# Graph attention on one core: a quarter of the weighting of gathered rows on ScalarE, with the weights in SBUF

## The chip, the core and the metric

The kernel runs on one core of one Trainium2 chip. A core has five engines with instruction queues of their own, each worked off in order: PE (TensorE: matrix products, with PEld for its weight loads), DVE (VectorE), ACT (ScalarE), POOL (GpSimd, which here issues the gathers by index) and SP (which here issues plain transfers). They wait for each other through semaphores. The metric is the device time of one execution in microseconds.

## The reference

One layer over 6250 nodes of 256 features, in three parts. The change lies in the first, a graph attention over 200 000 edges that are sorted by destination:

```python
z = jnp.einsum('ni,hid->nhd', h, W)              # 4 heads of 64
es = jnp.einsum('nhd,hd->nh', z, a_src)
ed = jnp.einsum('nhd,hd->nh', z, a_dst)
e = es[src] + ed[dst]
e = jnp.where(e >= 0, e, SLOPE * e)
ex = jnp.exp(e - m[dst])                         # m: maximum over a node's edges
alpha = ex / denom[dst]                          # denom: sum of ex over a node's edges
out = jax.ops.segment_sum(alpha[:, :, None] * z[src], dst, num_segments=N)
```

Added to it are the node itself and a linear attention of 8 heads over all nodes (the mixer). A second part follows: a second, narrow graph attention over 131 072 other edges gives scores, which choose two of four experts for each node.

## The kernel before

**Tiles.** Nodes lie in 49 tiles of 128. Edges lie in chunks of 128, one edge a partition, at fixed places: 33 chunks for each tile but the last, which has 28. That makes 1612 chunks, worked off in 202 groups of `G1 = 8`. The table `ztab` in HBM holds for each node its `z` with a 1 behind every head (4 x 65 columns, `ZW`) and four source terms.

**First edge stage.** The class `FirstEdges` holds the steps of one group. `gather` (L784) issues on POOL one indirect transfer for each chunk: by the row numbers in `src_c` (SBUF) it brings 128 rows of `ztab` into the tile `gt`, which takes `GH = 4` chunks; there are seven such tiles. `load` (L807) brings the destination numbers from SP's queue. `one_hot` (L813) and `one_hot_t` (L822) build, on DVE, the 0/1 matrices between edges and nodes. `terms` (L828) fetches the destination terms by PE; `terms_sum` (L836), `sources` (L798, then two exponentials on ACT, L213 and L214) and `weights` (L840, L842) make of them four weights for each edge, `wp`. This array lies in PSUM, in the tile `dv`, whose first 128 columns hold the numbers 0 to 127. `weigh` (L848) multiplies half a group's gathered rows, 4 chunks x 4 heads x 65 columns, by the weights on DVE, in place, and `add` (L857) sums the rows by destination on PE, into the PSUM tile `ag` of the node tile.

**Order.** The loop over the groups writes out the order of every engine's queue. For group g: gathers of g+2, `load` of g+3, `weights`, `weigh` of chunks 0 to 3, `terms` of g+1, `add` of chunks 0 to 3, `weigh` of chunks 4 to 7, `one_hot` of g+1, `add` of chunks 4 to 7, `one_hot_t` of g+2, `terms_sum` and `sources` of g+1. In six places between these, `mix_hops` puts in steps of the mixer and of the second layer norm, which use PE, DVE, ACT and SP. At the end of a group come steps of the sorting of the second part's edges (L381, L383, L413, L415 on DVE).

**Second stage.** The same pattern for the second attention (`SecondEdges`, gathers at L1321), between the experts' matrix products (L1427, L1447). It is not touched. Neither is the other use of `FirstEdges`, a branch for inputs whose tiles hold more edges than the fixed places; the inputs here don't take it.

Of the kernel before, what the change touches and what calls it, by code (L numbers as in the profile page):

```python
# [9 lines left out]
F32 = mybir.dt.float32  # L10
# [3 lines left out]
AF = mybir.ActivationFunctionType  # L14
# [6 lines left out]
P = 128  # L21
# [6 lines left out]
G1 = 8  # L28
GH = 4
K1, K1L = 33, 28  # L30

ZW = 4 * 65
# [32 lines left out]
def gps_layer(ctx: ExitStack, tc: tile.TileContext, a: dict, out: bass.AP):  # L65
    nc = tc.nc
    V, S, G, T, SP = nc.vector, nc.scalar, nc.gpsimd, nc.tensor, nc.sync
# [431 lines left out]
    with tc.tile_pool(name="a_x", bufs=1) as ax, tc.tile_pool(name="a_w", bufs=3) as aw, tc.tile_pool(  # L499
        name="a_p", bufs=2, space=PSUM  # L500
# [269 lines left out]
    class FirstEdges:  # L770
# [67 lines left out]
        def weights(self):  # L838
            n, pw = self.n, self.pw
            V.tensor_mul(pw[:, :n], pw[:, :n], self.sf[:, :n])  # L840
            self.wp = self.dv[:, P : P + 4 * G1].rearrange("p (c h) -> p c h", h=4)
            V.tensor_max(self.wp[:, :n], pw[:, :n, 0:4], pw[:, :n, 4:8])  # L842

        def weigh(self, c0, c1):
            if c0 < self.n:
                c1 = min(c1, self.n)
                gz = self.gt[c0 // GH][:, : c1 - c0, 0:ZW].rearrange("p c (h d) -> p c h d", h=4)
                V.tensor_mul(gz, gz, self.wp[:, c0:c1].unsqueeze(3).to_broadcast([P, c1 - c0, 4, 65]))  # L848

        def add(self, sums, s0, c0, c1):  # L850

# [184 lines left out]
    with tc.tile_pool(name="g1_w", bufs=2) as w, tc.tile_pool(name="g1_g", bufs=7) as gp, tc.tile_pool(  # L1036
        name="m_w", bufs=2
# [78 lines left out]
    with tc.If(many != 0):  # L1116
# [7 lines left out]
        with tc.tile_pool(name="sl_k", bufs=1) as k, tc.tile_pool(name="sl_w", bufs=1) as w, tc.tile_pool(  # L1124
            name="sl_p", bufs=1, space=PSUM
# [41 lines left out]
            with tc.For_i(0, NI, 1) as i:  # L1167
                c = nc.values_load(
                    l_c[0:1, ds(i, 1)], engines=(ENG.SP,), min_val=0, max_val=B1 * P - 1,
                    skip_runtime_bounds_check_because="numbers of chunks",  # L1170
                )
# [66 lines left out]
    with tc.tile_pool(name="d_k", bufs=1) as dk:  # L1238
# [3 lines left out]
        with tc.tile_pool(name="d_o", bufs=1) as do:  # L1242
# [5 lines left out]
            with tc.tile_pool(name="s2_p", bufs=1, space=PSUM) as ps1:  # L1248
                room = acc2.rearrange("p t f -> p (t f)")
                source_max(do, ps1, most_2, h_all[:, :, HW:HF], "f2")  # L1250
                d = room[:, : NT * 4].rearrange("p (t h) -> p t h", h=4)
# [454 lines left out]
        with tc.tile_pool(name="g2_w", bufs=2) as w, tc.tile_pool(name="g2_g", bufs=6) as gp, tc.tile_pool(  # L1706
            name="g2_p", bufs=1, space=PSUM
# [88 lines left out]
        with tc.If(bad != 0):  # L1796

            own_edges()
            with tc.tile_pool(name="h2_k", bufs=1) as hk, tc.tile_pool(name="h2_w", bufs=1) as w, tc.tile_pool(
                name="h2_p", bufs=1, space=PSUM  # L1800
# [60 lines left out]
```

## Time and profile before

Three timed runs: 3212.33, 3219.29 and 3220.07 us; median 3219.29. The profiled execution took 4023.54 us, with a span of 4021.7 us from the first to the last instruction.

| | busy in the profile, us | share of the span | instructions |
|---|---|---|---|
| PE | 2498.4 | 62% | 10919 |
| DVE | 2464.6 | 61% | 6571 |
| POOL | 2328.2 | 58% | 2436 |
| ACT | 506.5 | 13% | 1319 |

| steps of the first edge stage | engine | count | mean ns |
|---|---|---|---|
| `weigh` L848 | DVE | 403 | 1224 |
| `one_hot` L813 | DVE | 202 | 1208 |
| `add` L857, two products a chunk | PE | 3224 | 474 |
| `weights` L842 | DVE | 202 | 190 |
| exponentials L213, L214 | ACT | 201 each | 321, 214 |

The first gather of the first edge stage starts at 138.1 us, its last at 2614.0; the second stage's gathers run from 2642.2 to 3957.9. In the rows of the profile, a group of instructions is named by line, engine, operation and tiles (out<-in), followed by shapes and count, then busy time and mean duration, then the idle time of the engine before them and what ended it. A row of the timeline has start and length in microseconds first. POOL's row for a gather is the time in which it issues one, not the transfer.

### The profile page before, as it was taken

The page shows a single profiled execution, that of the slowest core. Times are in us where ns is not written, and L with a number is a line of the kernel's source. Part 1 is how long each engine was busy: PE and PEld are TensorE (multiplying, and loading weights), DVE is VectorE, ACT ScalarE, POOL GpSimd, SP SyncE. Part 2 cuts the span into 40 slices and gives each one's busy share as a digit, 9 for nine tenths or more (in the row PEclk, how much of TensorE's full clock was granted, in tenths as well). Part 3 has the DMA queues.
Part 4 walks back from the last instruction along what each step waited for, and adds up shares of the span by engine and source line. Part 5 has one row for each costly group of instructions (what it writes and reads, how often), then busy time and mean ns, then how long its engine had stood idle before and what let it go on. Part 6 is the DMA issues. An engine that isn't in the chain of part 4 may idle for free. (4 is left out here: it accounts for less than half of the span.)

```text
span 4021.7 us, 36890 instructions
## 1 busy us (share of the span) xinstructions
PE 2498.4 (62%) x10919; PEld 1773.3 (44%) x10920; DVE 2464.6 (61%) x6571; ACT 506.5 (13%) x1319; POOL 2328.2 (58%) x2436
## 2 busy tenths in 40 slices
PE   5666677755564555546555555446666767677766
PEld 4444565544443444434444433324444444444444
DVE  5566666677774776766677566625555546565657
ACT  2200011111110110111111111121111011111112
POOL 2466666665665666656666566655556556555552
PEclk8778798877776777777777777767888788888878
DMA  5443344444443443444444444332222123222221
GB/s 166 131 114 109 108 116 110 119 119 116 122 130 97 116 123 108 120 112 115 133 116 127 113 125 109 104 81 51 45 60 50 42 49 81 53 61 57 59 56 32
DMA packets 248565, 388.33 MB, mean 97 GB/s; under 512 B 73447, under 2 KB 156279, under 8 KB 248090
## 3 DMA queue, kind: packets, MB, share of 16 engines
q0 software_dynamic: 103296, 230.96, 23.1%
q1 hardware_dynamic: 142893, 154.04, 12.6%
q8 instruction: 91, 1.49, 0.1%
q14 instruction: 129, 1.05, 0.1%
q10 hardware_dynamic: 2156, 0.80, 0.1%
HBM read 345.44 MB, written 40.15 MB: 96 GB/s over the span
## 5 line engine op out<-in xcount | busy, mean ns | idle before, releaser
L784 POOL DMA_INDIRECT gt<-ztab,src_c x1612 | 1551.5, 962 | 967.3 <-issue 406.3
L857 PE MATMUL ag<-gt,oh 128*128 128x260 f32 x3224 | 1017.2, 474 | 342.6 <-DVE gt L848 232.0
L1321 POOL DMA_INDIRECT gt<-htab,src x784 | 748.6, 955 | 595.3 <-DVE dv L1390 261.2
L857 PEld LDWEIGHTS ag<-gt,oh 128*128 128x128 f32 x3224 | 754.0, 241 | 527.2 <-DVE gt L848 255.0
L1427 PE MATMUL hp<-xy,w 128*128 128x512 f32 (+1 forms) x832 | 444.3, 657 | 187.2 <-ACT hT L1432 140.5
L1447 PE MATMUL yo<-w,hT 128*128 128x256 f32 x1568 | 446.4, 425 | 111.4 <-issue 63.8
L848 DVE TENSOR_TENSOR gt<-gt,dv 128x1040 f32<-128x1040 f32 x403 | 489.0, 1224 | 13.7 <-issue 12.6
L1447 PEld LDWEIGHTS yo<-w,hT 128*128 128x128 f32 x1568 | 316.5, 209 | 246.2 <-issue 137.2
L883 PE MATMUL m<-wqkv,xy 128*128 128x256 f32 (+1 forms) x784 | 254.6, 464 | 169.5 <-DVE kmax L894 85.3
L1427 PEld LDWEIGHTS hp<-xy,w 128*128 128x128 f32 x832 | 169.0, 216 | 328.5 <-issue 167.3
L883 PEld LDWEIGHTS m<-wqkv,xy 128*128 128x128 f32 (+1 forms) x784 | 171.8, 231 | 217.2 <-DVE kmax L894 91.3
L813 DVE TENSOR_TENSOR oh<-dv,dl_c 128x1024 f32<-128x1024 f32 x202 | 244.0, 1208 | 7.8 <-PE ag L857 5.2
L1432 ACT ACTIVATE hT<-hp,b 128x512 f32<-128x512 f32 (+1 forms) x208 | 133.5, 660 | 479.4 <-remote 172.9
L1371 DVE TENSOR_TENSOR e_sel<-ed,ohq 128x384 f32<-128x384 f32 x98 | 54.1, 552 | 182.4 <-remote 136.8
L213 ACT ACTIVATE src_f<-src_d,shift_c 128x32 f32<-128x32 f32 x202 | 64.9, 321 | 772.5 <-DVE src_d L798 441.4
L381 DVE MAX8 src<-dl 128x8 f32<-128x1024 f32 x128 | 155.5, 1215 | 0.0
L383 DVE MATCH_REPLACE8 dl<-src,dl 128x1024 f32<-128x1024 f32 x127 | 153.5, 1209 | 0.0
L976 PE MATMUL m<-m_sb,qT 128*128 128x256 f32 (+1 forms) x196 | 74.4, 516 | 125.4 <-ACT qT L973 86.8
L1412 DVE TENSOR_REDUCE ag<-ag 128x40 f32<-128x120 f32 x98 | 27.2, 277 | 193.5 <-remote 154.5
L828 PE MATMUL ed<-pw,ohT 128*128 128x24 bf16 x1612 | 71.8, 176 | 106.7 <-DVE ohT L822 46.3
L828 PEld LDWEIGHTS <-ohT 128*128 128x128 bf16 x1612 | 67.1, 100 | 141.6 <-DVE ohT L822 53.6
L836 DVE TENSOR_REDUCE pw<-ed 128x64 f32<-128x192 f32 x202 | 69.6, 344 | 94.9 <-remote 74.6
(374 smaller groups left out, 2745.7 us busy)
## 6 DMA issues: line engine op xcount, KB each, us to landing
br<-rows SPq DMA_DIRECT2D x299, 256.0 KB
gt<-ztab,src_c POOLq DMA_INDIRECT x1612
gt<-htab,src POOLq DMA_INDIRECT x784
early<-ys SPq DMA_DIRECT2D x24, 512.0 KB
ys<-early SPq DMA_DIRECT2D x24, 512.0 KB
ztab<-zt SPq DMA_DIRECT2D x48, 132.0 KB
row<-in_x_dram SPq DMA_DIRECT2D x48, 128.0 KB
out_dram<-ys SPq DMA_DIRECT2D x47, 128.0 KB
```

Of the source, the lines that this page charges most:

```text
L381: V.max(out=srtf[:, 8 * i : 8 * i + 8], in_=keyf)
L383: V.match_replace(out=keyf, in_to_replace=srtf[:, 8 * i : 8 * i + 8], in_values=keyf, imm_value=0.0)
L784: G.indirect_dma_start(out=self.gt[-1][:, c % GH, :], out_offset=None, in_=ztab[:, :], in_offset=bass.IndirectOffsetOnAxis(ap=self.idx[:, ...
L813: V.tensor_tensor(self.oh[:, :n], self.dv[:, None, :P].to_broadcast([P, n, P]), self.dl[:, :, None].to_broadcast([P, n, P]), op=OP.is_equal,)
L828: T.matmul(self.ed[:, c, :], self.ohT[:, c * P : (c + 1) * P], pw3[:, ds(self.tiles[c], 1), :].rearrange("p a b -> p (a b)"), start=True, ...
L848: V.tensor_mul(gz, gz, self.wp[:, c0:c1].unsqueeze(3).to_broadcast([P, c1 - c0, 4, 65]))
L857: T.matmul(sums[t], self.oh[:, c], self.gt[c // GH][:, c % GH, 0:ZW], start=(s0 + c == 0 or chunk_tile[s0 + c - 1] != t), stop=last,)
L883: T.matmul(out_, xy[:, t, j, :n], wqkv[:, j, c0 : c0 + D], start=(j == 0), stop=(j == 1))
L1321: G.indirect_dma_start(out=self.gt[:, c, : tab.shape[1]], out_offset=None, in_=tab[:, :], in_offset=bass.IndirectOffsetOnAxis(ap=self.idx[ ...
L1427: T.matmul(hp[:, :m], wts[e][0][:, c, j * P : (j + 1) * P], xy[:, t0 : t0 + nt, c] if m == nt * P else xy[:, t0, c, :m], start=(c == 0), s ...
L1432: S.activation(h[:, :m], hp[:, :m], AF.Gelu, bias=b1[:, e, j : j + 1])
L1447: T.matmul(yo[:n], hT[j][:, o : o + n], wts[e][1][:, j, :], start=(j == 0 and e < EARLY), stop=(j == 3))
```

## The change

Two edits in `FirstEdges`. The weights `wp` move from PSUM into an SBUF tile of their own, a single buffer. And `weigh` leaves the last chunk of every full half to ACT: DVE multiplies three chunks in one instruction (780 columns), ACT the fourth in four instructions, one for each head (65 columns, with the weight of the head as the scale of a `Copy` activation). All 403 halves are full, so ACT gets 1612 instructions.

```diff
         def weights(self):
             n, pw = self.n, self.pw
             V.tensor_mul(pw[:, :n], pw[:, :n], self.sf[:, :n])
-            self.wp = self.dv[:, P : P + 4 * G1].rearrange("p (c h) -> p c h", h=4)
+            self.wp = self.w.tile([P, G1, 4], F32, name="wp", bufs=1)
             V.tensor_max(self.wp[:, :n], pw[:, :n, 0:4], pw[:, :n, 4:8])
 
         def weigh(self, c0, c1):
+
             if c0 < self.n:
                 c1 = min(c1, self.n)
-                gz = self.gt[c0 // GH][:, : c1 - c0, 0:ZW].rearrange("p c (h d) -> p c h d", h=4)
-                V.tensor_mul(gz, gz, self.wp[:, c0:c1].unsqueeze(3).to_broadcast([P, c1 - c0, 4, 65]))
+                gt, m = self.gt[c0 // GH], min(c1 - c0, GH - 1)
+                gz = gt[:, :m, 0:ZW].rearrange("p c (h d) -> p c h d", h=4)
+                V.tensor_mul(gz, gz, self.wp[:, c0 : c0 + m].unsqueeze(3).to_broadcast([P, m, 4, 65]))
+                if c1 - c0 == GH:
+                    for h in range(4):
+                        gh = gt[:, m, 65 * h : 65 * (h + 1)]
+                        S.activation(gh, gh, AF.Copy, scale=self.wp[:, c1 - 1, h : h + 1])
```

## The prediction

> **What bounds the kernel now.** I read the page's costliest groups first, then the busy time by stretch, then the line of the gathers, then the timeline.
>
> ```profile
> L784 POOL DMA_INDIRECT gt<-ztab,src_c x1612 | 1551.5, 962 | 967.3 <-issue 406.3
> ...
> L1321 POOL DMA_INDIRECT gt<-htab,src x784 | 748.6, 955 | 595.3 <-DVE dv L1390 261.2
> ...
> L848 DVE TENSOR_TENSOR gt<-gt,dv 128x1040 f32<-128x1040 f32 x403 | 489.0, 1224 | 13.7 <-issue 12.6
> ```
>
> The change touches L848, 489 us of DVE, and nothing of POOL. But look at POOL: 1612 gathers in the first edge stage, 784 in the second. The median gather takes 949 ns and the next starts 1254 ns after it did: 305 ns lie between two however ready everything is (the rows below say "0.30 <-issue"). By the mean, one costs 0.962 + 0.305 = 1.267 us in the first stage and 0.955 + 0.305 = 1.260 in the second: 2042 + 988 = 3030 us that no other engine can shorten.
>
> ```profile
> 138.00:2615.00 2477.00, 1446.88 (x6411) 1118.84 (x6412) 1631.19 (x4098) 272.82 (x779) 1551.45 (x1612) 0.76 0.42 117
> 2642.00:3959.00 1317.00, 918.45 (x3870) 555.25 (x3871) 697.18 (x1942) 167.12 (x331) 748.65 (x784) 0.81 0.25 58
> ```
>
> Columns: stretch, length, then busy us of PE, PEld, DVE, ACT, POOL, the granted clock, DMA. In the profiled execution (span 4021.7, its own time 4023.5) the first stage lasts 2477, so POOL waits 2477 - 2042 = 435 us there, mostly for PE to free a `gt` buffer. That execution is 804 us longer than the 3219 median. I added up the stretches of over 2 us in which PE, DVE and ACT all stand still while POOL goes on gathering: 116 of them, 601 us. So most of the excess is standstill of the computing engines. What the timed runs leave outside the gathers is 3219 - 3030 = 189 us, and the profiled one needs 138 before the first gather, 27 between the stages and 63 after the last: 228. The gathers' sequence fills the timed run entirely: **POOL's gather pace is the bound**, and DVE, 1631 us busy in a stage of 2042, has some 410 us to spare (2.0 us a group of eight chunks).
>
> **What the weights' move does to POOL.** This is the part that decides. L848 multiplies `gt` (SBUF) by `dv` (PSUM); after the change both inputs lie in SBUF. The trace has DVE instructions of that kind: L968, L996, L999, L1001.
>
> ```profile
> 1054.17 0.95 POOL L784 DMA_INDIRECT gt<-ztab,src_c  x1 [0.30 <-issue]
> 1055.38 0.42 DVE L1001 TENSOR_TENSOR kx<-kx,row 128x256 f32<-128x256 f32 x1
> 1055.42 1.20 POOL L784 DMA_INDIRECT gt<-ztab,src_c  x1 [0.30 <-DVE row L999]
> ```
> ```profile
> 1479.54 3.00 POOL L784 DMA_INDIRECT gt<-ztab,src_c  x1 [0.31 <-DVE yb L995]
> 1479.63 0.74 DVE L996 TENSOR_TENSOR yb<-yb,gamma 128x256 f32<-128x256 f32 x2
> 1480.31 0.74 DVE L999 TENSOR_TENSOR row<-yb,row 128x256 f32<-128x256 f32 x2
> 1480.98 0.74 DVE L1001 TENSOR_TENSOR kx<-kx,row 128x256 f32<-128x256 f32 x2
> ```
> ```profile
> 1511.68 1.23 DVE L848 TENSOR_TENSOR gt<-gt,dv 128x1040 f32<-128x1040 f32 x1
> 1511.76 0.95 POOL L784 DMA_INDIRECT gt<-ztab,src_c  x1 [0.30 <-issue]
> ```
>
> Each row: start, length. A gather that starts just after such an instruction ends 0.82 us after it (1055.80 + 0.82 = 1056.62), not 0.95 after its own start; behind six in a row it takes 3.00 us. Beside today's L848 it takes 0.95. I counted over the trace, by what DVE ran 0.13 us into the gather (0.95 - 0.82): under L968, L999 and L1001, 23 of 25 gathers took over 965 ns; under L848, 1 of 306; under L813, PSUM against SBUF too, 2 of 132. L968 is even the new form, a tensor times a broadcast, and 8 of its 9 blocked.
>
> The new L848 has 780 elements, not 1040. From 1040 in 1224 ns and 256 in 416 (L968) the slope is 1.03 ns, so 416 + 524 x 1.03 = 956 ns. A gather is blocked if it starts within the first 956 - 130 = 826 ns of it. Gathers start every 1254 ns: 0.66 of the multiplications catch one, and hold it 413 ns on average, so 0.272 us each; x403 = **110 us more on POOL**. Bounds: 0 if they always fell between two reads, 403 x 0.826 = 333 if they always caught one at its start. The phase wanders with the mixer's and sorting work between, so I take the even spread. 77 of the 201 pairs of L848 follow each other within 0.1 us today; there one gather may wait through both, as in the 3.00 us row, which pulls upward (two windows of 0.83 become one of some 1.7, costing 1.08 instead of 0.54: up to 77 x 0.54 = 42). Below zero is excluded: L848 costs POOL nothing today.
>
> Here a rule is to be weighed. The Trainium skill, "SBUF — State Buffer", section "Who interferes with whom", says that a DVE instruction with two SBUF inputs contends with a GpSimd instruction that reads SBUF, not with one that only writes, and that a `tensor_tensor` did not stall a DMA issued there, because descriptor generation wants the write interface. By that last sentence the sum is 0; by its first, with a gather that reads its row numbers from `src_c` in SBUF, it is 110. The 23 of 25 decide for the first.
>
> **DVE's part.** 403 x (1224 - 956) = 108 us less DVE. None of it is on the path while POOL paces: it lengthens DVE's waits for landed chunks. L842, which writes the weights, already reads two SBUF operands; SBUF instead of PSUM as its output is worth at most some 20 of its 190 ns, x202 = 4 us either way, in the same spare time.
>
> **ACT's part.** 1612 multiplications of 128x65, four per half. Nearest rows:
>
> ```profile
> L213 ACT ACTIVATE src_f<-src_d,shift_c 128x32 f32<-128x32 f32 x201 | 64.6, 321 | 771.7 <-DVE src_d L798 440.6 <-issue 77.8 <-DVE ohT L822 49.2
> L214 ACT ACTIVATE src_f<-src_d 128x32 f32<-128x32 f32 x201 | 43.0, 214 | 0.0
> ...
> L1541 ACT ACTIVATE dg<-ident,gate 128x128 f32<-128x128 f32 x4 | 1.5, 398 | 2.4 <-PE yo L1542 1.5 <-DVE gate L1692 0.9
> ```
>
> L1541 is the same function with its scale read per partition: 398 ns for 128 columns, so 321 to 398, some 350 for 65. Two of them back to back took 0.69, so one every 0.29: four take 0.35 + 3 x 0.29 = 1.2 us, 490 us in all, on an engine busy 273 of 2042. "ScalarE: Activation LUTs", section "Rules for kernel authors", puts multiplications on VectorE, and by engine time it is right: DVE saves 0.27 us a half, ACT spends 1.2. On the path it would add 403 x 0.9 = 360; it isn't there: ACT starts when the weights stand, beside DVE's 0.96, and PE (1017.2 us / 1612 = 0.63 a chunk) reaches the fourth chunk 1.9 us after DVE is done. L1541 follows an exponential with no table load between, so the table loads (30 and 30 in this stage) stay.
>
> **New waits.** (1) The fourth chunk's matmul waits for ACT; behind it on PE stand the mixer's matmuls. Covered by the 1.9 us. If ACT is held by a mixer copy that itself waits for PE (L173 waited 113.7 us in 21 cases), the cover is gone for that group, at about 1.2 us. (2) `wp` is a single buffer: the next group's L842 on DVE now waits until ACT has read the last weights. Behind it queue the multiplication and the one-hot, and PE waits for both. Between lie the one-hot (1.21), `ohT` (0.48) and mostly two sort steps (2.4) against ACT's 1.2. (3) The exponentials of the next group's `src_f` come behind ACT's four. All three eat the 2.0 us of a group first, while POOL may run up to seven `gt` tiles (28 chunks, 35 us) ahead. I take 0; at 1.2 us a group with no spare left they cost 240. DMAs, SP's queue and the second stage are unchanged.
>
> **Sum.** 3219 + 110 + 0 = 3329 us. The profiled execution has 435 us of POOL waits to soak the blocking up, so its span should grow less than 110.
>
> **Rivals.** (a) *DVE's relief wins.* If the timed stage were paced by DVE, and POOL faster unprofiled than 1.25 us, 108 us go: 3111 at best, 3165 with half on the path. For it: in the profile POOL does wait for PE, and PE for L848 (232 us). Against: the 189 against 228 us above. (b) *Half hidden.* POOL's timed pace leaves some slack, and half of the 110 vanishes in it: 3219 + 55 = 3274. For it: the 228 came out above 189, so the timed pace may be a little shorter than the profiled. (c) *The ACT chain bites.* Blocking plus new waits once the 2.0 us of a group are spent, at half of the 240: 3329 + 120 = 3449. (d) *Nothing shows*, 3219: slack swallows all; it needs over 110 us of POOL idle in the timed stage.
>
> **Chances.** Forecast case 0.67 (its own range 3290 to 3385, from 70 to 165 us of blocking), (b) 0.13, (c) 0.05, (d) 0.05, (a) 0.10. A measurement of this kernel tells some 0.3%, 10 us, from no change. Faster 0.10, same 0.05, slower 0.85. For 8 in 10 the range runs from 3235, which takes in (b), to 3390; outside lie (a), (c) and (d), 0.20 together.
>
> **What would show it.** L784's mean rises from 962 ns to about 1030 (962 + 110/1612) with many gathers of 1.2 to 1.8 us that end 0.82 us after an L848-like multiplication; that row falls to some 956 ns; 1612 ACT rows near 350 ns. Gathers at 949 beside the new multiplication would break the argument; so would a stage that shrinks by DVE's 108 us.

## The result and the profile after

Three timed runs of the changed kernel took 3305.38, 3313.07 and 3321.05 us: median 3313.07, **1.0306 of the time before (95% interval 1.0285 to 1.0326)**, so 94 us slower. The forecast was 3329 us. The profiled execution took 3305.38 us, with a span of 3303.6.

In the runs below, every version of this kernel took about 4.0 ms on two chips and about 3.2 on two others, and the profile shown of before is of the first sort, while the timed runs and the profile of after are of the second. So the two spans (4021.7 and 3303.6) don't measure the change. The stretches of over 2 us in which PE, DVE and ACT all stand still sum to 150 us in after (44 of them), against the 601 of before. What can be compared is how long an instruction takes, and what it collides with.

The page's costliest groups of the changed kernel, in the columns used before (the multiplication on DVE is now L850, the one on ACT L854, the second stage's gathers L1327):

```profile
L784 POOL DMA_INDIRECT gt<-ztab,src_c x1612 | 1641.1, 1018 | 519.1 <-issue 386.2
...
L1327 POOL DMA_INDIRECT gt<-htab,src x784 | 748.4, 955 | 264.2 <-issue 208.8
L854 ACT ACTIVATE gt<-gt,wp 128x65 f32<-128x65 f32 x1612 | 414.5, 337 | 339.7 <-DVE wp L842 252.3
L798 DVE TENSOR_TENSOR src_d<-gt,most 128x16 f32<-128x16 f32 x403 | 67.1, 171 | 519.5 <-DMA gt<-ztab,src_c 514.7
...
L850 DVE TENSOR_TENSOR gt<-gt,wp 128x780 f32<-128x780 f32 x403 | 380.1, 958 | 0.1
```

Four things are to be seen. The multiplication fell to 958 ns. ACT's 1612 instructions take 337 ns each. The gathers of the first stage, which nobody edited, rose from a mean of 962 to 1018 ns: 89.6 us more POOL time, while those of the second stage stand at 955 as before. And DVE waits 514.7 us at L798 for chunks to land, where before's profile has 8.6 us of such waits: DVE is far from being the limit here.

Busy time by stretch (stretch, length, busy us of PE, PEld, DVE, ACT, POOL, granted clock, DMA share, GB/s):

```profile
113.00:2256.00 2143.00, 1401.31 (x6414) 1104.63 (x6414) 1529.42 (x4111) 674.16 (x2382) 1641.09 (x1612) 0.81 0.49 135
2283.00:3257.00 974.00, 837.54 (x4046) 530.46 (x4046) 719.46 (x2020) 179.46 (x359) 738.41 (x774) 0.95 0.34 79
```

In the first stage POOL's 1641.1 us of gathers and some 0.305 us after each (1612 x 0.305 = 492) make 2133 of 2143 us. **POOL is never idle but for 10 us.** This is the "timed" stage that the prediction had to infer, and it paces as inferred.

Two stretches of the timeline of after show the mechanism (start, length; the bracket is the idle time before):

```profile
1018.99 0.95 POOL L784 DMA_INDIRECT gt<-ztab,src_c  x1 [0.30 <-issue]
...
1019.11 1.81 DVE L850 TENSOR_TENSOR gt<-gt,wp 128x780 f32<-128x780 f32 x2
...
1020.24 1.50 POOL L784 DMA_INDIRECT gt<-ztab,src_c  x1 [0.30 <-DVE gt L850]
...
1022.05 0.94 POOL L784 DMA_INDIRECT gt<-ztab,src_c  x1 [0.30 <-issue]
```
```profile
1010.14 0.94 POOL L784 DMA_INDIRECT gt<-ztab,src_c  x1 [0.30 <-DVE gt L850]
1010.19 0.96 DVE L850 TENSOR_TENSOR gt<-gt,wp 128x780 f32<-128x780 f32 x1
```

Two multiplications run from 1019.11 to 1020.92. The gather of 1018.99 had a start of 0.12 us on them and takes its 0.95. The next begins at 1020.24, inside the second, and ends at 1021.74: 1020.92 + 0.82, the figure that the prediction took from the mixer's rows. At 1010.14 a lead of 0.05 us was enough to slip past. Over the whole stage I counted the gathers that start within a multiplication, at least 130 ns ahead of its end: 183 of the 403 multiplications have one, and 178 of the 183 gathers take over 965 ns. In before it was 1 of 305.

### The profile page after: what moved, and what is told of

It is laid out like the page before. It is cut to its first block, busy times and chain, and to the rows that moved or that the text cites. A ratio compares the mean times of both kernels' runs of the same rounds, so it can differ in the third digit from the quotient of the medians.

```text
span 3303.6 us, 39715 instructions
## 1 busy us (share of the span) xinstructions
PE 2340.1 (71%) x10919; PEld 1710.5 (52%) x10920; DVE 2355.8 (71%) x6571; ACT 908.1 (27%) x2931; POOL 2418.2 (73%) x2436
## 5 line engine op out<-in xcount | busy, mean ns | idle before, releaser
L784 POOL DMA_INDIRECT gt<-ztab,src_c x1612 | 1641.1, 1018 | 519.1 <-issue 386.2
L863 PE MATMUL ag<-gt,oh 128*128 128x260 f32 x3224 | 995.4, 467 | 318.1 <-DVE gt L850 301.4
L1327 POOL DMA_INDIRECT gt<-htab,src x784 | 748.4, 955 | 264.2 <-issue 208.8
L854 ACT ACTIVATE gt<-gt,wp 128x65 f32<-128x65 f32 x1612 | 414.5, 337 | 339.7 <-DVE wp L842 252.3
L798 DVE TENSOR_TENSOR src_d<-gt,most 128x16 f32<-128x16 f32 x403 | 67.1, 171 | 519.5 <-DMA gt<-ztab,src_c 514.7
L1453 PE MATMUL yo<-w,hT 128*128 128x256 f32 x1568 | 396.5, 396 | 51.5 <-DVE ys L1496 51.5
L1433 PE MATMUL hp<-xy,w 128*128 128x512 f32 (+1 forms) x832 | 402.4, 609 | 20.0 <-ACT hT L1438 16.1
L850 DVE TENSOR_TENSOR gt<-gt,wp 128x780 f32<-128x780 f32 x403 | 380.1, 958 | 0.1
L1453 PEld LDWEIGHTS yo<-w,hT 128*128 128x128 f32 x1568 | 291.1, 194 | 153.0 <-DVE ys L1496 76.8
L813 DVE TENSOR_TENSOR oh<-dv,dl_c 128x1024 f32<-128x1024 f32 x202 | 244.6, 1211 | 11.7 <-PE ag L863 11.4
L1386 DVE TENSOR_TENSOR pr<-pw,gt 128x64 f32<-128x64 f32 x98 | 22.0, 224 | 230.2 <-DMA gt<-htab,src 154.6
L1348 DVE TENSOR_TENSOR oh<-dv,dl 128x1024 bf16<-128x1024 f32 x98 | 119.0, 1214 | 0.0
```

Source lines behind the costliest of these rows:

```text
L784: G.indirect_dma_start(out=self.gt[-1][:, c % GH, :], out_offset=None, in_=ztab[:, :], in_offset=bass.IndirectOffsetOnAxis(ap=self.idx[:, ...
L813: V.tensor_tensor(self.oh[:, :n], self.dv[:, None, :P].to_broadcast([P, n, P]), self.dl[:, :, None].to_broadcast([P, n, P]), op=OP.is_equal,)
L850: V.tensor_mul(gz, gz, self.wp[:, c0 : c0 + m].unsqueeze(3).to_broadcast([P, m, 4, 65]))
L854: S.activation(gh, gh, AF.Copy, scale=self.wp[:, c1 - 1, h : h + 1])
L863: T.matmul(sums[t], self.oh[:, c], self.gt[c // GH][:, c % GH, 0:ZW], start=(s0 + c == 0 or chunk_tile[s0 + c - 1] != t), stop=last,)
L1327: G.indirect_dma_start(out=self.gt[:, c, : tab.shape[1]], out_offset=None, in_=tab[:, :], in_offset=bass.IndirectOffsetOnAxis(ap=self.idx[ ...
```

## Experiments

The theory: two SBUF operands on DVE hold a gather, and POOL paces. The rivals: the split itself costs (ACT's chain, waits on the single weights tile), or DVE's relief has an effect of its own. Each ratio is to the kernel before on the same chip. "Held by it" sums what gathers starting in the multiplication take beyond 947 ns.

| kernel | before there, us | this, us | ratio (95%) | L784 mean ns | multiplication ns, weights in | caught gathers, held | held by it, us |
|---|---|---|---|---|---|---|---|
| `e3_two_copies` | 3990.74 | 3991.01 | 1.0012 (0.9988 to 1.0037) | 957 | 953, PSUM | 223, 0 | 0 |
| `e2_sbuf_dve` | 3990.74 | 3946.12 | 0.9899 (0.9852 to 0.9945) | 1056 | 1228, SBUF | 272, 268 | 152.1 |
| `e4_two_on_act` | 3990.74 | 4004.27 | 1.0066 (1.0035 to 1.0096) | 993 | 688, SBUF | 143, 134 | 43.0 |
| `e5_one_column` | 3990.74 | 3945.97 | 0.9898 (0.9852 to 0.9944) | 962 | 171, PSUM | 9, 0 | 0 |
| `f1_two_copies` | 3205.96 | 3200.51 | **0.9983** (0.9977 to 0.999) | 959 | 952, PSUM | 285, 0 | 0 |
| `f2_sbuf_dve` | 3205.96 | 3352.77 | **1.046** (1.044 to 1.048) | 1050 | 1227, SBUF | 284, 279 | 140.7 |
| `g1_port_free` | 4017.13 | 4068.83 | 1.0103 (1.0043 to 1.0163) | 952 | 952, PSUM | 202, 0 | 0 |
| `g3_one_column` | 4017.13 | 3976.17 | 0.9893 (0.986 to 0.9926) | 962 | 170, PSUM | 7, 0 | 0 |
| `g4_two_on_act` | 4017.13 | 4041.06 | 1.0064 (1.0042 to 1.0087) | 993 | 686, SBUF | 143, 138 | 42.9 |
| `h1_changed` | 3207.44 | 3317.05 | **1.0333** (1.0317 to 1.0349) | 1026 | 958, SBUF | 197, 192 | 93.0 |
| `h2_port_free` | 3207.44 | 3194.21 | **0.9954** (0.9941 to 0.9968) | 955 | 955, PSUM | 281, 0 | 0 |

### Undo one part: the split stays, DVE reads its weights in PSUM

ACT still does a quarter, with the single weights tile in SBUF; DVE gets a copy of its own in PSUM.

```diff
-            self.wp = self.w.tile([P, G1, 4], F32, name="wp", bufs=1)
+            self.wa = self.w.tile([P, G1, 4], F32, name="wa", bufs=1)
+            self.wp = self.dv[:, P : P + 4 * G1].rearrange("p (c h) -> p c h", h=4)
             V.tensor_max(self.wp[:, :n], pw[:, :n, 0:4], pw[:, :n, 4:8])
+            V.tensor_copy(self.wa[:, :n], self.wp[:, :n])
...
-                        S.activation(gh, gh, AF.Copy, scale=self.wp[:, c1 - 1, h : h + 1])
+                        S.activation(gh, gh, AF.Copy, scale=self.wa[:, c1 - 1, h : h + 1])
```

> The split stays (three chunks on DVE, the fourth on ACT), but DVE reads its weights from PSUM again; ACT reads a second copy in SBUF, one more small DVE copy a group. Port theory (the blocked gathers are the whole loss): no gather is held by the three-chunk multiplication, L784's mean returns from 1018 to about 962 ns, and the time to 3219 within 10 us; DVE's 108 us less are worth nothing. ACT rival (the loss is new waits on ACT): stays near 3313. Relief rival (DVE's 108 us are worth something and the blocking ate more than it shows): under 3200.

> Again the split with weights for DVE in PSUM and a copy for ACT in SBUF, hoped for in an execution of 3219 us for the kernel before, where the gathers pace the first stage (where PE, DVE and ACT stand still for hundreds of microseconds and the kernel before takes 3990, POOL waits anyway and the time tells nothing of it: then no change). Port theory: no gather is held by the three-chunk multiplication, ratio 1.00 within 0.003. ACT rival: ratio 1.03, as the changed kernel. Relief rival: under 0.99.

`e3` came out at no difference, but on a chip where POOL has hundreds of microseconds to spare, so that it decides little about the time. `f1`, on a chip like that of the timed runs, decides: 0.9983. Its groups (the multiplication is L852):

```profile
L784 POOL DMA_INDIRECT gt<-ztab,src_c x1612 | 1545.6, 959 | 509.1 <-issue 375.3
...
L852 DVE TENSOR_TENSOR gt<-gt,dv 128x780 f32<-128x780 f32 x403 | 378.0, 952 | 0.0
```

and its timeline, a gather in the midst of two multiplications:

```profile
1021.65 1.83 DVE L852 TENSOR_TENSOR gt<-gt,dv 128x780 f32<-128x780 f32 x2
...
1021.77 1.07 ACT L856 ACTIVATE gt<-gt,wa 128x65 f32<-128x65 f32 x4 [2.65 <-DVE wa L844]
...
1022.05 0.95 POOL L784 DMA_INDIRECT gt<-ztab,src_c  x1 [0.30 <-issue]
```

The same work of the same length, one operand in another memory, and the gather takes 0.95 us. Against this kernel the loss of the change can be read off two rows: L784 busy 1641.1 - 1545.6 = 95.5 us, idle before it 519.1 - 509.1 = 10.0, together 105.5; the two spans differ by 3303.6 - 3200.5 = 103.1. All that the split brings with it (1612 ACT instructions, the single tile, ACT's queue order) is in `f1` too, and costs nothing there on balance: between two gathers of its first stage POOL never waits longer than the usual 0.3 us.

### Do one part alone: the weights move, DVE keeps all four chunks

```diff
-            self.wp = self.dv[:, P : P + 4 * G1].rearrange("p (c h) -> p c h", h=4)
+            self.wp = self.w.tile([P, G1, 4], F32, name="wp", bufs=1)
```

> The weights' move alone: DVE multiplies all four chunks, weights from SBUF, nothing on ACT. Port theory: the instruction lasts 1224 ns instead of 958 and is open to a hit for 1094 ns instead of 828; the stall goes with the square, so 84 us x (1094/828)^2 = 147 us, about 3370 us, and L784's mean rises to about 1055 ns. ACT rival: 3219.

> Again the weights' move alone, all four chunks on DVE. Port theory, where the gathers pace the stage: 152 us of blocking, as the trace of the run before this showed, all of it on the path: 3219 + 152 = 3371 us, ratio 1.047. ACT rival: ratio 1.00. Where the kernel before takes 3990 and POOL waits anyway: 0.99, as before.

```profile
L784 POOL DMA_INDIRECT gt<-ztab,src_c x1612 | 1693.2, 1050 | 506.3 <-issue 385.4
...
L848 DVE TENSOR_TENSOR gt<-gt,wp 128x1040 f32<-128x1040 f32 x403 | 490.4, 1227 | 0.1
```

These are the groups of `f2`: the multiplication is as long as before, and L784 alone has grown, by 147.6 us over `f1`, with its idle time 2.8 us shorter. That is 144.8 us together, and the spans are 146.0 apart; over before the time grew by 146.8. One line of the change carries the whole loss, and more of it than the change shows, since the longer instruction catches more gathers. `e2` has even more of the holds (152.1 us) and is not slower at all, but 1.0% faster: there the idle time before L784 is 764.3 us, against 964.1 in `e3`, so the holds went into time in which POOL would have waited anyway:

```profile
L784 POOL DMA_INDIRECT gt<-ztab,src_c x1612 | 1702.9, 1056 | 764.3 <-issue 417.4
```
```profile
L784 POOL DMA_INDIRECT gt<-ztab,src_c x1612 | 1542.5, 957 | 964.1 <-issue 433.7
```

These are the rows of `e2` and of `e3`. The holds cost only where POOL paces. The 1.0% that `e2` gains on top is not explained: its multiplication is as long as before, so no DVE time is saved.

### Vary the dose: two chunks on ACT

```diff
-                gt, m = self.gt[c0 // GH], min(c1 - c0, GH - 1)
+                gt, m = self.gt[c0 // GH], min(c1 - c0, GH - 2)
...
-                    for h in range(4):
-                        gh = gt[:, m, 65 * h : 65 * (h + 1)]
-                        S.activation(gh, gh, AF.Copy, scale=self.wp[:, c1 - 1, h : h + 1])
+                    for c in range(m, GH):
+                        for h in range(4):
+                            gh = gt[:, c, 65 * h : 65 * (h + 1)]
+                            S.activation(gh, gh, AF.Copy, scale=self.wp[:, c0 + c, h : h + 1])
```

> The changed kernel with two of four chunks on ACT, eight instructions a half. Port theory: DVE's instruction has 520 elements, about 690 ns, open for 560: 84 x (560/828)^2 = 38 us of stall, so 3219 + 38 + 10 = 3267 us; L784's mean about 985 ns. ACT rival: the ACT chain doubles, 3400 us.

> The changed kernel with two of four chunks on ACT. Port theory, where the gathers pace the stage: 43 us of stall as its trace showed, all of it on the path: ratio 1.013 to 1.017. ACT rival: the loss grows beyond the changed kernel's 1.03.

By the even spread, a multiplication of D us holds gathers for (D - 0.130)²/(2 x 1.254) on average. Times 403, the sizes 688, 958 and 1228 ns give 50, 110 and 194 us; measured were 43, 83 to 93, and 141 to 152. So the growth is there, a little less steep than the square, at 0.73 to 0.86 of its size. (The 43 and the 152 come from 4.0 ms executions, in which gathers start less often.) In time, both runs were 0.6% slower on chips where before takes 4.0 ms. There the holds can hide and 3224 ACT instructions (806.8 us) are in play; what makes the 0.6% isn't settled. What two chunks on ACT cost where POOL paces, for which 1.013 to 1.017 was expected, was not measured.

### Does DVE's relief alone bring anything?

`weigh` multiplies only the 65th column of each head, so 1024 of 1040 products are left out.

```diff
-                V.tensor_mul(gz, gz, self.wp[:, c0:c1].unsqueeze(3).to_broadcast([P, c1 - c0, 4, 65]))
+                V.tensor_mul(gz[:, :, :, 64:65], gz[:, :, :, 64:65], self.wp[:, c0:c1].unsqueeze(3).to_broadcast([P, c1 - c0, 4, 1]))
```

> The kernel before with nearly all of the multiplication left out: of the 65 columns of a head only the last (the denominators) is multiplied, 16 elements in place of 1040, weights in PSUM; 1024 of 1040 products are not computed. DVE loses some 403 x 1.06 = 427 us. If POOL's gathers pace the stage: 3219 within 15 us. If DVE paces it: down to 2800, half of that on the path 3005.

> The kernel before with 1024 of 1040 products of the weighting left out (weights in PSUM), DVE 427 us lighter. If the gathers pace the stage: ratio 0.995 to 1.002. If DVE does: 0.87, half of it on the path 0.93.

L848 fell to 171 ns, 424 us less DVE work, and both came out 1.0 to 1.1% faster, 41 to 45 us, on chips where before takes 4.0 ms. In such an execution DVE is thus, for the most part, not the limit either. It was not run on a chip of the other sort; what stands for the timed runs is `f1`, with 403 x (1224 - 952) ns less multiplication and some 36 us more copying (202 x 0.18), in sum 74 us less DVE, and a time 5.5 us shorter.

### A version without either kind of hold

In the trace of before a second kind of instruction stood over held gathers: L822, the comparison with one number per partition, which reads and writes SBUF alone (of the 58 gathers that start in it, at least 130 ns ahead of its end, 45 took over 965 ns). This version has DVE's weights in PSUM as in `f1`, and L822 as a tensor against a PSUM column (the lines of `f1`, and the same two lines in the branch that isn't taken, are left out here):

```diff
-            V.tensor_scalar(self.ohT[:, :m], self.br[:, :m], part, None, op0=OP.is_equal)
+            V.tensor_tensor(
+                self.ohT[:, :m], self.dv[:, P + 4 * G1 :].to_broadcast([P, m]), self.br[:, :m], op=OP.is_equal
+            )
...
-        dv = ps.tile([P, P + 4 * G1], F32, name="dv", bufs=1)
+        dv = ps.tile([P, P + 4 * G1 + 1], F32, name="dv", bufs=1)
         V.tensor_copy(dv[:, :P], lane)
+        V.tensor_copy(dv[:, P + 4 * G1 :], part)
```

> An attempt to beat both: the two copies of the weights, and in the first stage the transposed one-hot (L822) too reads one operand from PSUM (the partition number, as a tensor) in place of a scalar compare of SBUF alone. In the run with two copies L822 ended 27 held gathers, 4.1 us. Port theory, where the gathers pace the stage: these holds go, 4 us less than two copies, ratio to before 0.997; DVE pays for it with an instruction of some 1210 ns in place of 484, 202 x 0.73 = 147 us, out of the 108 it was spared and its spare time. Rival (DVE's time matters after all): slower than before.

> Again the version with two copies and the transposed one-hot's operand in PSUM. Where the gathers pace the stage: ratio to before 0.997 (4 us less than two copies alone). Where the kernel before takes about 4000 us: 1.01, as before.

> The changed kernel itself, unedited, beside the others. Port theory, where the kernel before takes about 3210 us and the gathers pace it: ratio 1.03 as measured first. Where the kernel before takes about 4000 us, since PE, DVE and ACT stand still so often that POOL waits anyway: the holds of the gathers vanish in POOL's waits, ratio 0.995 to 1.005, with L784's mean near 1018 ns all the same.

The groups of `h2`:

```profile
L784 POOL DMA_INDIRECT gt<-ztab,src_c x1612 | 1540.0, 955 | 509.1 <-issue 373.2
...
L822 DVE TENSOR_TENSOR ohT<-dv,br 128x1024 bf16<-128x1024 f32 x202 | 244.6, 1211 | 0.0
```

L822 now takes 1211 ns, where before's profile has 0.48 us: about 147 us more DVE work. And yet `h2` is **faster than both kernels**, 0.9954 of before and 3194.21 / 3317.05 = 0.963 of the changed one on the same chip, with L784 5.6 us shorter than in `f1`; the gain over before is a little more than the expected 0.997. Where POOL paces, DVE time is cheap and a held gather is dear. On a chip where before takes 4.0 ms the same kernel is 1.0% slower (`g1`), the mirror of `e5`: there less DVE work gains a little, more of it costs a little, and fewer holds gain nothing.

### The kernel before, once more

> The kernel before, unedited, for its trace in an execution near 3210 us. Port theory: POOL waits under 20 us for anything in either stage, against 434 and 329 us in the profile shown; L784's mean near 960 ns; DVE waits for landed chunks by the hundred us. DVE rival: POOL waits for PE or DVE by the hundred us here too.

It was to give a profile of before in an execution of about 3.2 ms. It took 4014.73 us, with L784 at 963 ns, so such a profile is missing, and `f1` stands in for it. What makes the 4.0 ms stays open.

## Why the prediction was right

**The bound** was right. It was read from an execution 804 us longer than the timed ones, by the sum of pitches. The changed kernel's first stage shows POOL busy for all but 10 us of it, and `f1`'s gathers take 2036.3 us from first start to last end, 1.263 us each, against the 1.267 taken; its second stage takes 987 us, against 988. Two readings on the way were loose and changed nothing: of the 434 us that POOL waits in the profile of before, the rows put 167 down to the sums on PE (L857), the largest part but not most, and 106 of the 116 standstills (575 of the 601 us), not all, have a gather in them.

**The hold** was right in kind: rows with ends 0.82 us after the multiplication, L784 at 1018 to 1026 ns against "about 1030", 958 ns for the multiplication against 956. (L996, named with the three lines of the count and left out of it, held 4 of 6.) `f1` and `f2` show it to be the cause by taking it away and by doing it alone. Of what the prediction took from the Trainium skill, "SBUF — State Buffer", section "Who interferes with whom", the rule on two SBUF inputs agrees with these runs, and the remark on `tensor_tensor` and DMA issue does not hold for these gathers by index: 178 of 183 were held.

**Its size** was too large by a quarter: 82.9 us in the profiled execution (93.0 in `h1`) instead of 110. The mis-sized term is the share of multiplications that catch a gather: 183 of 403, 0.45, instead of 0.66. The mean hold was 0.47 us, not 0.413, which gave back a part. The even spread itself came out about right; what the sum left out is that a held gather keeps the next one away. Of the 220 multiplications without a gather, 119 begin while one is still being held, in 104 cases by an earlier multiplication, so that no other can start in their first part. Of the remaining 284, 183 catch one: 0.64. In `h1` it is 197 of 279, 0.71, and in `f2` 284 of 324, 0.88, where the even spread gives (1227 - 130)/1254 = 0.87. One such pair in the timeline of after:

```profile
651.84 1.84 DVE L850 TENSOR_TENSOR gt<-gt,wp 128x780 f32<-128x780 f32 x2
...
652.01 1.61 POOL L784 DMA_INDIRECT gt<-ztab,src_c  x1 [2.09 <-issue]
```

The first multiplication ends at 652.80 and the gather 0.82 us later, at 653.62. The next gather starts 0.31 us after that, at 653.93, when the second multiplication is over (653.68). So the pull upward from adjacent pairs was the wrong way round: 100 of the 201 pairs follow within 0.1 us in after, in none of them do both catch a gather, and such a pair costs one hold.

**What the sum lacked**: some 12 us more of holds by other DVE instructions than in `f1` (L822 with 9.2 instead of 5.2 us, the layer norm's rows most of the rest), and 10 us in which POOL waits, which I had put at zero. Those waits of 1.5 to 2.2 us lie between 540 and 680 us. One of them in the timeline of after:

```profile
648.46 0.37 ACT L928 COPY vt<-m 128x256 f32<-128x256 f32 x1 [1.07 <-DVE kq L927]
648.73 0.42 ACT L929 ACTIVATE kq<-kq 128x256 f32<-128x256 f32 x1
648.98 0.94 POOL L784 DMA_INDIRECT gt<-ztab,src_c  x1 [1.47 <-ACT vt L928]
649.05 2.02 ACT L854 ACTIVATE gt<-gt,wp 128x65 f32<-128x65 f32 x8
```

ACT's eight multiplications stand behind the mixer's copy and activation, much as the new wait (1) had it, and POOL stood for 1.47 us until, by the profile, ACT's copy released it. Of the seven waits the profile names a releaser for this one alone, so ACT as their cause is argued. `h1` has such waits too (14 us), while neither `f1` nor `f2` has one over 0.05 us, so it takes the split and the holds together; more than that was not tried. In sum 83 + 12 + 10 = 105 over `f1`, which is itself 5.5 us under before: about 100, where the medians of the two comparisons give 94 and 110. That the forecast of 110 comes so close is in part luck: a hold taken too large by 17 to 27 us made up for terms set at nothing.

**DVE and ACT.** DVE's 108 us were worth nothing on the path, as taken: `f1` has most of them and gains 5.5 us. L842 went from 190 to 181 ns, within the 20 taken. ACT's instructions took 337 ns instead of 350, 414.5 us instead of 490, and cost nothing by themselves (`f1`), where they would have added the estimated 360 had ACT been on the path. The rule of the Trainium skill that multiplications go to VectorE ("ScalarE: Activation LUTs", section "Rules for kernel authors") hardly mattered to this time (`f1`: 0.9983).

**The rivals.** *DVE's relief wins* falls with `f1`, *the ACT chain bites* too, but for the 10 us. *Half hidden* and *nothing shows* fall with `f2`, where the span grew by as much as the gathers did. On the chips of 4.0 ms, though, `e2` is what *nothing shows* described: the holds are swallowed by POOL's idle time.

## What to carry over

Find the engine that paces in the *timed* execution, by pitch times count if the profile is of a longer one, and weigh each edit by what it does to that engine: here 74 us less on DVE went with a gain of 5.5, and one operand in another memory cost 147. Where gathers issued on POOL pace, keep one operand of DVE's long instructions in PSUM, and count a move of small operands to SBUF as a cost that grows somewhat less than with the square of the instruction's length, since an instruction that follows closely on another often finds POOL still held. An edit with two parts has to be measured part by part: the split was harmless and only looked bad beside the weights' move.

## What the hardware showed beyond this

- An instruction with one SBUF tensor can hold gathers too: of the gathers that start in the bf16 comparison L822, 31 of 39 took over 965 ns in `f1`, and 1 of 166 once it read a PSUM operand (`h2`).
- ACT's multiplications, which read SBUF for data and scale, hold none: of the 327 gathers that start in one of the 1612 in `h2`, four took over 965 ns, and each of these four ends 0.82 us after a DVE instruction with two SBUF tensors.
- The signs of small edits turn about with whether the gathers pace: moving the weights alone gives +4.6% where before takes 3.2 ms and -1.0% where it takes 4.0 (`f2`, `e2`), the version without holds -0.5% and +1.0% (`h2`, `g1`).
